# Scaled operands left in pieces between later products, with T2 and T4 kept negated, in a two-level Winograd graph layer

## The chip, the cores and the metric

The kernel runs on one core of a Trainium2 chip. The metric is the device time in microseconds (us) of one execution; lower is better. The profile is of a single execution, taken by the hardware profiler. Five engines work beside each other: TensorE (PE, with its weight loads as PEld), VectorE (DVE), ScalarE (ACT), GpSimd (POOL) and SyncE (SP). Each works through its own instructions in order, and semaphores hold an instruction until what it needs is there. In this kernel SP issues loads, and POOL issues stores and a few small loads besides its own sums.

## The reference

Two graph layers on x (4096 x 512) with one matrix adj (4096 x 4096), all in float32:

```
# layer 0
mask = (adj > 0); head = mask / max(sqrt(row sum of mask), 1e-12)
inc  = adj + head
x1   = layernorm(x + (inc @ x) / rowsum(inc))
# layer 1
A2   = adj + I;  d = diag(A2) ** -0.5
temp = A2 @ x1 @ W.T
out  = layernorm(x1 + relu(d * (A2 @ (d * temp))))
```

So there are three large products (inc @ x, A2 @ x1 and A2 @ (d * temp)) and one small one, the projection by W.T, which stands between the second and the third.

## The kernel before, in words

**Large products.** Layer 0 uses Winograd's form of Strassen's scheme on one level, and the two products with A2 use it on two levels. The code numbers them k = 2 (A2 @ x1) and k = 3 (A2 @ (d * temp)). On the outer level the left matrix is cut in quarters and the right matrix, 4096 x 512, in quarters B11, B12, B21, B22 of 2048 x 256. Seven outer products p = 1 to 7 are made, for each of two column stretches s of the result (s = 0, 1), in the order of `ORDER` (L179): 4, 5, 1, 6, 7, 2, 3 for k = 2 and 2, 3, 5, 1, 6, 7, 4 for k = 3. Each outer product takes one right operand out of seven (`OPERAND`, L181): B11, B21, B22 or one of the sums

```
T1 = B11 - B12      T2 = -T1 - B22      T3 = B22 - B12      T4 = B21 + T2
```

The right operands lie in HBM, in the tiles `outer_b[k]`, until `load_b` (L247) fetches them in groups for two steps; `sum_b` (L253) makes the inner sums of a group.

**Steps.** An outer product is eight steps, kk = 0 to 7. A step is seven inner products (`multiply2`, L273), each of four matmuls of 128 x 512 and each into its own PSUM bank (0 to 6); the eighth bank is the spare. The main loop (L993 to L1061) emits, for each step: the left sums for the step two later (`prepare`, on DVE), every second step the right sums (`sum_b`, DVE), pieces of the projection, the seven products, loads, and what follows the products. After kk = 7, `outer` (L701) evicts the seven banks by way of `inner` (L680): ACT copies bank q1 to p1 (L684) and q5 to p5 (L687), DVE does the rest (L685 to L692) and adds into the outer results c11, c12, c21, c22. The next outer product writes the same banks again from its first step on, so its first inner product needs the copy L684 and its second one needs L685.

**Projection.** When half of the rows of A2 @ x1 (h = 1 or h = 0) is complete for a stretch s, four calls of `project` (L750) are put in the list `pairs`, and they are worked off two in each of the next two outer products. A call handles two row blocks of 128 rows (r = 0 and 1). The first call of an outer product starts at kk = 2 (here "the early block"), the second at kk = 4 ("the late block"). Each makes seven small products with W in the spare bank (L766), put between the inner products of a step; ACT copies each out (L768) before the next can start, since there is only one spare bank. POOL makes the sums of the left side (L773 to L776). The early block has its small products in the steps kk = 2, 3 and 4, the late block in 4, 5 and 6. Then DVE adds them up (L795 to L801) into two tiles `z` (a ring of two, one for each row block, holding `first` and `second`, the left and right half of the 512 columns) and into one tile `t` (a single buffer) with t = first - second of both row blocks (L804). The late block of an outer product writes the same two `z` and the same `t` that the early block had.

**Leaving.** `leave_operands` (L809) scales `first`, `second` and `t` by d on ACT (L816) and stores them from POOL (L819, L826) as right operands of k = 3. The rows of h = 1 come first: they write B21 and B22, and T2, T3, T4 with what of them comes from these rows. The rows of h = 0 come later: they write B11 and T1, and accumulate their part into T2, T3 and T4 in HBM. Both row blocks leave at once, right after the DVE sums: after kk = 4 for the early block and after kk = 6 for the late block. A block of h = 1 takes six scalings and eight transfers, a block of h = 0 eight scalings and ten transfers. A second `t` place, `m`, holds the negated copy that T2 and T4 want.

**Order.** The schedule is written by hand: the engines run in the order in which the loop emits their instructions. Pools give a tile's buffer again only when all its readers are done, transfers that read it among them.

There are eight outer products with a pair of projection blocks in them. In this document they are E, F (h = 1, s = 0), A, B (h = 0, s = 0), G, H (h = 1, s = 1) and C, D (h = 0, s = 1), in the order of time E, F, A, B, G, H, C, D.

Of the kernel before, what the change touches and what calls it, by code (L numbers as in the profile page):

```python
# [10 lines left out]
AF = mybir.ActivationFunctionType  # L11
ALU = mybir.AluOpType

P = 128
# [6 lines left out]
B11, B21, B22, T1, T2, T3, T4 = range(7)  # L21
# [5 lines left out]
def tile_adj_resnorm_d2(  # L27
# [37 lines left out]
    nc = tc.nc  # L65
    N, D = x.shape
    H = D // 2
# [9 lines left out]
    NQ = NB // 4  # L77
    SW = 512
    NS = NQ * P // SW
    SB = SW // P  # L80
# [14 lines left out]
    def spare():  # L95
        return bank(7)
# [15 lines left out]
    dscale = const.tile([P, NB], F32, name="dscale")  # L112
    nscale = const.tile([P, NB], F32, name="nscale")
# [22 lines left out]
    def in_outer(k, j, ops):  # L136

        kk, half = j % NQ, j // NQ
        ap = outer_b[k][kk // 2][ops, kk % 2, :, 2 * half:2 * half + 2, :]
        return ap.rearrange("o p q d -> p o (q d)")  # L140

    def split(y):
        return y.rearrange("p (o d) -> p o d", o=2)
# [48 lines left out]
    completed = set()  # L192
    resident, loaded, ready, raw_b, sums_b = {}, {}, {}, {}, {}
    made = {"a": 0, "s": 0, "load": 0, "load_b": 0}
    going = []
    queue, pairs, later, deferred, raises = [], [], [], [], []

    def fresh():
# [102 lines left out]
    chunks, sums, slots, counts, scale, natural = {}, {}, {}, {}, {}, {}  # L301
# [328 lines left out]
    for n in range(NC, NP * NC):  # L630
        j, c = divmod(n, NC)
# [62 lines left out]
    def add(o, y):  # L694
        nc.vector.tensor_add(o, o, y)

    def less(o, y, z):

        nc.vector.scalar_tensor_tensor(o, y, -1.0, z, op0=ALU.mult, op1=ALU.subtract)

    def outer(k, p, acc):  # L701

        (c11, c12), (c21, c22) = C_of[k]

        def into(dst):
            inner(acc, lambda i, op: op(dst[:, i, :]))

        def by_way(then):
            def put(i, op):
                y = row_tile("y", 2)  # L710
                op(y)
                then(i, y)
            inner(acc, put)

        if k == 2:
            if p in (4, 5, 1):
                into({4: c21, 5: c22, 1: c11}[p])
            elif p == 6:
                into(c12)
                deferred.extend((lambda: add(c12, c11), lambda: nc.vector.tensor_sub(c21, c21, c12),  # L720
                                 lambda: add(c12, c22)))
            elif p == 7:
                into(c22)
                deferred.extend((lambda: nc.vector.tensor_sub(c21, c21, c22), lambda: less(c22, c22, c12)))
            else:
                dst = {2: c11, 3: c12}[p]
                by_way(lambda i, y: add(dst[:, i, :], y))
        else:
            if p in (2, 3):
                into({2: c11, 3: c12}[p])  # L730
            elif p == 5:
                into(c22)
                deferred.append(lambda: add(c12, c22))
            elif p == 1:
                into(c21)
                deferred.append(lambda: add(c11, c21))
            elif p == 6:
                by_way(lambda i, y: add(c21[:, i, :], y))
                deferred.append(lambda: add(c12, c21))
            elif p == 7:  # L740
                by_way(lambda i, y: add(c21[:, i, :], y))
                deferred.append(lambda: less(c22, c22, c21))
            else:
                by_way(lambda i, y: nc.vector.tensor_sub(c21[:, i, :], y, c21[:, i, :]))

    def blocks(h, s):

# [2 lines left out]
    def project(h, s, n, first):  # L750

        cols = slice(n * P, (n + 1) * P)
        a11, a12, a21, a22 = (C_of[2][h][f][:, 2 * r:2 * r + 2, cols] for r in range(2) for f in range(2))
        if first:
            pools["places"] = [t[:, i * H:(i + 1) * H] for t in (row_tile(t, 1) for t in ("p1", "p5", "u2", "u3")) for i in range(2)]

        places = [pools["places"][i] for i in (range(7) if first else (7, 1, 0, 6, 3, 2, 4))]
        q = []  # L760

        def product(left, right):
            def now():
                ps = spare()[:, 0:H]
                for e in range(2):
                    nc.tensor.matmul(ps, left[:, e, :], wt[:, right, e, :], start=(e == 0), stop=(e == 1))  # L766
                q.append(places[len(q)])
                nc.scalar.copy(q[-1], ps)  # L768
            return now

        def sums():
            s1, s2, s3, s4 = (y[:, 2 * i:2 * i + 2, :] for y in (row_tile("y", 2, (P, 4, P)) for _ in range(2)) for i in range(2))
            nc.gpsimd.tensor_add(s1, a21, a22)  # L773
            nc.gpsimd.tensor_add(s2, a11, s1)
            nc.gpsimd.tensor_add(s3, a11, a21)
            nc.gpsimd.tensor_add(s4, a12, s2)  # L776
            return s1, s2, s3, s4

        if first:
            yield {1: product(a11, B11), 3: product(a12, B21), 5: product(a22, T4)}  # L780
            s1, s2, s3, s4 = sums()
            yield
            yield {1: product(s2, T2), 3: product(s3, T3), 5: product(s1, T1)}
            yield
            yield {1: product(s4, B22)}
        else:
            yield {4: product(a11, B11)}
            s1, s2, s3, s4 = sums()
            yield
            yield {1: product(a12, B21), 3: product(a22, T4), 5: product(s2, T2)}  # L790
            yield
            yield {1: product(s3, T3), 3: product(s1, T1), 5: product(s4, B22)}
        q1, q2, q4, q6, q7, q5, q3 = q
        z = [row_tile("z", 2) for _ in range(2)]
        nc.vector.tensor_add(z[0][:, 0:H], q2, q1)  # L795
        nc.vector.tensor_add(q6, q6, q1)
        nc.vector.tensor_add(q7, q7, q6)
        nc.vector.tensor_add(q6, q6, q5)
        nc.vector.tensor_add(z[0][:, H:D], q3, q6)
        nc.vector.tensor_sub(z[1][:, 0:H], q4, q7)  # L800
        nc.vector.scalar_tensor_tensor(z[1][:, H:D], q7, -1.0, q5, op0=ALU.mult, op1=ALU.subtract)  # L801
        t = row_tile("t", 1, (P, 4, H))
        for r in range(2):
            nc.vector.tensor_sub(t[:, 2 * r, :], z[r][:, 0:H], z[r][:, H:D])  # L804
        for r in range(2):
            leave_operands(h, r * NQ + s * SB + n, z[r], t[:, 2 * r, :], t[:, 2 * r + 1, :])
        yield

    def leave_operands(h, j, z, t, m):  # L809

        b = j + h * NP

        def scaled(o, y, by=dscale):
            nc.scalar.activation(o, y, AF.Copy, scale=by[:, b:b + 1])  # L816

        def put(op, y, **how):
            nc.gpsimd.dma_start(out=in_outer(3, j, slice(op, op + 1)), in_=y.unsqueeze(1), **how)  # L819

        first, second = z[:, 0:H], z[:, H:D]
        if h:
            scaled(m, second, nscale)
            scaled(z, z)
            scaled(t, t)
            nc.gpsimd.dma_start(out=in_outer(3, j, slice(B21, B22 + 1)), in_=split(z))  # L826
            put(T2, m)
            put(T3, second)
            put(T4, t)
        else:  # L830
            scaled(m, t, nscale)
            scaled(t, t)
            scaled(first, first)
            scaled(second, second, nscale)
            put(B11, first)
            put(T1, t)
            put(T2, m, accum_op=ALU.add)
            put(T3, second, accum_op=ALU.add)
            put(T4, m, accum_op=ALU.add)

    def turn_back(ps, at, h, r, cols, fs):

# [52 lines left out]
    def finish(h, items, acc):  # L895


        c21 = C_of[3][h][0]
# [11 lines left out]
        def put(i, op):  # L910
            y = row_tile("y", 2)
            op(y)
            nc.vector.tensor_sub(c21[:, i, :], y, c21[:, i, :])

        def turn(t):
            j, r, cols = items[t]
# [76 lines left out]
    for n, (k, s, p, kk) in enumerate(steps):  # L993
# [15 lines left out]
        between = {3: lambda: take_up(items.pop(0))} if len(items) > 1 else {}  # L1009
        if kk in (2, 4) and pairs:  # L1010
            going.append(project(*pairs.pop(0), kk == 2))
        for pair in going:
            between.update(next(pair))
        if n < len(steps) - TAIL:
            multiply2(n, acc, between)
        if n == 0:
# [15 lines left out]
            next(pair)  # L1032
        if kk in (4, 6):
            del going[:1]
        if 1 <= kk <= (6 if end else 5):
            for kind, args in queue[:2]:
                fetch(kind, *args)
        if kk == NQ - 1 and n + 1 < len(steps):
            outer(k, p, acc)
            if (k, p) in DONE:  # L1040
                h = DONE[k, p]
# [8 lines left out]
                fetch(kind, *args)  # L1050
        while raises:
            raises.pop(0)()
        if n + 1 == len(steps) // 2:

            scope.close()
            ring3 = ctx.enter_context(tc.tile_pool(name="ring3", bufs=2))
            late["pool"] = ctx.enter_context(tc.tile_pool(name="late", bufs=1))
            i = made["a"] % 4
            pools["turn"] = [ring3] * 2 + pools["turn"][i:] + pools["turn"][:i]
            made["a"] = 0  # L1060
            PF = 3  # L1061
# [36 lines left out]
```

## Time and profile before

| What | Value |
|---|---|
| median of three executions | 2285.16 us (2283.39 to 2285.18) |
| the profiled execution, its own time | 2284.03 us |
| its span, first to last instruction | 2282.1 us |
| granted TensorE clock, mean | 0.998 |
| PE busy | 2255.1 us, 99% |
| DVE busy | 1854.4 us, 81% |
| ACT busy | 417.3 us, 18% |
| POOL busy | 383.3 us, 17% |
| moved by DMA | 555.80 MB, mean 244 GB/s |
| outer products with a projection | from 1058 to 1682 us |

The profile counts an engine as busy while it executes, and "idle before" is the time for which it stood still before an instruction, with the one that released it behind the arrow. PE is busy nearly throughout, so a time is changed only by what makes PE stand still, or by what takes matmuls away. A time on another engine counts only where PE, in the end, waits for it.

### The profile page before, as it was taken

Reading aid. Unit: us, or ns where it says so; the run is one execution under the profiler, and the core shown is the slowest. Engines: PE = TensorE matmul, PEld = TensorE weight load, DVE = VectorE, ACT = ScalarE, POOL = GpSimd, SP = SyncE. Lnnn points to the kernel's source line nnn. Section 1 sums busy time; section 2 is a strip of 40 time slices with the busy share of each in tenths; the row PEclk is TensorE's granted clock in tenths of the full one; section 3 lists DMA queues with packets and bytes.
Section 4 is the critical chain, followed back from the end, with each engine's and each line's share of the span. In section 5 each row is a group of like instructions: output and inputs, shape, how many; then the busy total and the mean of one; then the engine's idle time right before and its main releaser. Section 6 shows DMA issues by size and latency. Waiting matters only on the chain.

```text
span 2282.1 us, 22004 instructions
## 1 busy us (share of the span) xinstructions
PE 2255.1 (99%) x7359; PEld 1380.3 (60%) x7359; DVE 1854.4 (81%) x2619; ACT 417.3 (18%) x991; POOL 383.3 (17%) x548
## 2 busy tenths in 40 slices
PE   8999999999999999999999999999999999999997
PEld 6888888888888844444555444555544444444443
DVE  6988988988988777788876778887666788776788
ACT  4333223332232000000222100122110011100013
POOL 0111112211111110001333300232320000100013
PEclk9999999999999999999999999999999999999999
DMA  9788777878777576575767857576785676766573
GB/s 330 274 287 262 260 233 270 272 262 270 238 240 239 187 266 259 198 283 184 270 240 227 262 209 271 191 283 261 209 256 218 220 258 241 253 238 227 209 269 117
DMA packets 155936, 555.80 MB, mean 244 GB/s; under 512 B 17920, under 2 KB 32272, under 8 KB 117424
## 3 DMA queue, kind: packets, MB, share of 16 engines
q1 hardware_dynamic: 114624, 417.38, 51.6%
q0 software_dynamic: 41200, 137.03, 18.2%
q8 instruction: 58, 0.95, 0.2%
q14 instruction: 54, 0.44, 0.1%
HBM read 434.78 MB, written 119.55 MB: 243 GB/s over the span
## 4 chain that ended last, share of the span: by engine, by line
PE 89%; DVE 5%; DMA 3%; ACT 2%; issue 1%; POOL 0%; SPq 0%; DVEq 0%; ACTq 0%
PE q L278 55%; PE q L472 27%; PE q L766 3%; PE q L485 2%; DMA nat<-adj 2%; DVE s L167 1%; PE q L908 1%; PE q L844 1%; DVE s L169 0%; ACT z L816 0%; ACT nat L332 0%; DVE a L442 0%; DVE mask L435 0%; ACT t L816 0%; DVE ts L257 0%
## 5 line engine op out<-in xcount | busy, mean ns | idle before, releaser
L278 PE MATMUL q<-s,ts 128*128 128x512 f32 x1326 | 612.2, 592 | 0.1
L472 PE MATMUL q<-b,s 128*128 128x256 f32 (+1 forms) x1920 | 454.4, 379 | 0.0
L278 PEld LDWEIGHTS q<-s,ts 128*128 128x128 f32 x1326 | 251.6, 190 | 299.1 <-issue 268.3
L167 DVE TENSOR_TENSOR s<-a 128x1024 f32<-128x1024 f32 x236 | 290.2, 1230 | 161.4 <-PE q L278 131.3
L472 PEld LDWEIGHTS q<-b,s 128*128 128x128 f32 x1920 | 363.1, 189 | 53.1 <-DVE z L510 0.5
L472 PE MATMUL q<-b,a 128*128 128x258 f32 (+1 forms) x1440 | 352.5, 380 | 0.7 <-ACT p L503 0.6
L278 PE MATMUL q<-a,tr 128*128 128x512 f32 x692 | 329.4, 592 | 1.8 <-DMA a<-adj_r 1.8
L472 PEld LDWEIGHTS q<-b,a 128*128 128x128 f32 x1440 | 272.5, 189 | 40.9 <-ACT p L503 1.5
L278 PE MATMUL q<-s,tr 128*128 128x512 f32 x442 | 225.7, 592 | 0.0
L278 PEld LDWEIGHTS q<-a,tr 128*128 128x128 f32 x692 | 129.5, 190 | 145.1 <-issue 138.9
L332 ACT ACTIVATE nat<-nat,tiny 128x512 f32<-128x512 f32 x240 | 170.9, 714 | 235.9 <-DMA nat<-adj 235.7
L278 PE MATMUL q<-a,ts 128*128 128x512 f32 x346 | 176.8, 592 | 0.0
L169 DVE TENSOR_TENSOR s<-a,s 128x512 f32<-128x512 f32 x236 | 167.7, 711 | 8.1
L170 DVE TENSOR_TENSOR s<-a,s 128x512 f32<-128x512 f32 x236 | 167.3, 709 | 8.0
L442 DVE TENSOR_TENSOR a<-a,mask 128x1024 f32<-128x1024 f32 x123 | 150.7, 1225 | 6.6 <-DVE mask L435 0.5
L435 DVE SCALAR_TENSOR_TENSOR mask<-a,sc 128x1024 f32<-128x1024 f32 (+2 forms) x129 | 154.1, 1196 | 2.1
L278 PEld LDWEIGHTS q<-s,tr 128*128 128x128 f32 x442 | 84.0, 190 | 92.1 <-issue 84.6
L684 ACT COPY p<-q 128x512 f32<-128x512 f32 x27 | 15.6, 577 | 631.5 <-PE q L278 631.5
L278 PEld LDWEIGHTS q<-a,ts 128*128 128x128 f32 x346 | 65.7, 190 | 83.0 <-issue 76.1
L425 POOL DMA_DIRECT2D oa<-sr x64 | 57.7, 902 | 283.8 <-DVE sr L416 181.6
L873 POOL DMA_DIRECT2D out<-o x24 | 13.1, 547 | 507.8 <-ACT o L162 507.8
L278 PE MATMUL q<-r,tr 128*128 128x512 f32 x192 | 92.7, 593 | 0.0
(193 smaller groups left out, 2129.4 us busy)
## 6 DMA issues: line engine op xcount, KB each, us to landing
a<-adj_r SPq DMA_DIRECT2D x112, 1024.0 KB, 6.6
a<-oa SPq DMA_DIRECT2D x80, 1024.0 KB, 5.3
nat<-adj SPq DMA_DIRECT2D x240, 256.0 KB, 7.4
a<-adj_q SPq DMA_DIRECT2D x60, 1024.0 KB, 6.2
tr<-ob SPq DMA_DIRECT2D x112, 512.0 KB, 4.0
oa<-sr POOLq DMA_DIRECT2D x64, 512.0 KB, 7.2
oa<-r POOLq DMA_DIRECT2D x32, 1024.0 KB, 9.2
y<-x POOLq DMA_DIRECT2D x64, 256.0 KB, 7.2
```

Source lines behind the costliest of these rows:

```text
L167: nc.vector.tensor_add(s[:, S3:S1 + 1, :], a[:, A11:A22 + 1, :], a[:, A21, :].unsqueeze(1).to_broadcast([P, 2, w]))
L169: nc.vector.tensor_add(s[:, S2, :], a[:, A11, :], s[:, S1, :])
L170: nc.vector.tensor_add(s[:, S4, :], a[:, A12, :], s[:, S2, :])
L278: nc.tensor.matmul(acc[m], left, right, start=(kk == 0), stop=(kk == NQ - 1))
L332: nc.scalar.activation(y, a, AF.Sign, bias=tiny, scale=2.0 ** 64, accum_out=accum)
L425: nc.gpsimd.dma_start(out=dst, in_=sr.rearrange("p m (k i) -> p (m k) i", i=P))
L435: nc.vector.scalar_tensor_tensor(m, v, 0.0, s.unsqueeze(1).to_broadcast(list(v.shape)), op0=ALU.is_gt, op1=ALU.mult)
L442: nc.vector.tensor_add(z, z, y)
L472: nc.tensor.matmul(acc[m][:, 0:w], left, b[:, right, 0:w], start=(kk == 0), stop=(kk == NP - 1))
L485: nc.tensor.matmul(y[:, 0:w], left, slots[kk][:, op, 0:w], start=(kk == 0 and left is k1), stop=(kk == NP - 1 and left is k2))
L766: nc.tensor.matmul(ps, left[:, e, :], wt[:, right, e, :], start=(e == 0), stop=(e == 1))
L844: nc.tensor.transpose(ps[:, at + i * P:at + (i + 1) * P], C_of[3][h][d // 2][:, 2 * r + d % 2, cols], ident)
```

## The change

The scaling and the transfers are taken out of the projection's last piece and put in a list, `leaving`, with one entry for each row block. An entry is taken off at four places of the loop: during kk = 5 and during kk = 7 ahead of the seventh inner product, after kk = 5, and at the end of kk = 7 behind `outer`. So the early block leaves in and after kk = 5 instead of after kk = 4, and the late block in kk = 7, with its second row block behind the eviction of the banks, instead of after kk = 6.

T2 and T4 are stored with the opposite sign. Then `second` serves T2 and T3 of h = 1 as it is, and `t` serves T1, T2 and T4 of h = 0 as it is: the negated copy `m` and its scaling go, and one transfer with a repeated source writes two operands. A block of h = 1 has four scalings and six transfers, a block of h = 0 six scalings and eight transfers (seven for two row blocks, one of each half). The bytes of the operands stay the same. Where the outer products p = 6 and p = 4 of k = 3 are added up, the sign is taken back: an addition becomes a subtraction, and y - c becomes -y - c.

```diff
-    going = []
+    going, leaving = [], []
 ...
             elif p == 6:
-                by_way(lambda i, y: add(c21[:, i, :], y))
+                by_way(lambda i, y: nc.vector.tensor_sub(c21[:, i, :], c21[:, i, :], y))
 ...
             else:
-                by_way(lambda i, y: nc.vector.tensor_sub(c21[:, i, :], y, c21[:, i, :]))
+                by_way(lambda i, y: less(c21[:, i, :], y, c21[:, i, :]))
 ...
-        for r in range(2):
-            leave_operands(h, r * NQ + s * SB + n, z[r], t[:, 2 * r, :], t[:, 2 * r + 1, :])
+        leaving.extend(lambda r=r: leave_operands(h, r * NQ + s * SB + n, z[r], t[:, 2 * r, :]) for r in range(2))
         yield
 
-    def leave_operands(h, j, z, t, m):
+    def leave_operands(h, j, z, t):
 ...
-        def scaled(o, y, by=dscale):
-            nc.scalar.activation(o, y, AF.Copy, scale=by[:, b:b + 1])
+        def scaled(y, by):
+            nc.scalar.activation(y, y, AF.Copy, scale=by[:, b:b + 1])
 
-        def put(op, y, **how):
-            nc.gpsimd.dma_start(out=in_outer(3, j, slice(op, op + 1)), in_=y.unsqueeze(1), **how)
+        def put(ops, y, **how):
+            o = in_outer(3, j, ops)
+            nc.gpsimd.dma_start(out=o, in_=y.unsqueeze(1).to_broadcast([P, o.shape[1], H]), **how)
 
         first, second = z[:, 0:H], z[:, H:D]
         if h:
-            scaled(m, second, nscale)
-            scaled(z, z)
-            scaled(t, t)
+            scaled(z, dscale)
+            scaled(t, nscale)
             nc.gpsimd.dma_start(out=in_outer(3, j, slice(B21, B22 + 1)), in_=split(z))
-            put(T2, m)
-            put(T3, second)
-            put(T4, t)
+            put(slice(T2, T3 + 1), second)
+            put(slice(T4, T4 + 1), t)
         else:
-            scaled(m, t, nscale)
-            scaled(t, t)
-            scaled(first, first)
-            scaled(second, second, nscale)
-            put(B11, first)
-            put(T1, t)
-            put(T2, m, accum_op=ALU.add)
-            put(T3, second, accum_op=ALU.add)
-            put(T4, m, accum_op=ALU.add)
+            scaled(t, dscale)
+            scaled(first, dscale)
+            scaled(second, nscale)
+            put(slice(T1, T1 + 1), t)
+            put(slice(B11, B11 + 1), first)
+            put(slice(T2, T4 + 1, 2), t, accum_op=ALU.add)
+            put(slice(T3, T3 + 1), second, accum_op=ALU.add)
 ...
@@ finish, put @@
-            nc.vector.tensor_sub(c21[:, i, :], y, c21[:, i, :])
+            less(c21[:, i, :], y, c21[:, i, :])
 ...
@@ main loop @@
         for pair in going:
             between.update(next(pair))
+        if kk in (5, 7) and leaving:
+            between[6] = leaving.pop(0)
         if n < len(steps) - TAIL:
             multiply2(n, acc, between)
 ...
         if kk in (4, 6):
             del going[:1]
+        if kk == 5 and leaving:
+            leaving.pop(0)()
 ...
         while raises:
             raises.pop(0)()
+        if kk == NQ - 1 and leaving:
+            leaving.pop(0)()
```

## The prediction

> **What bounds the kernel now.** I read the page first, then the waits of TensorE, then the timelines of single stretches.
>
> ```profile
> PE 2255.1 (99%) x7359; PEld 1380.3 (60%) x7359; DVE 1854.4 (81%) x2619; ACT 417.3 (18%) x991; POOL 383.3 (17%) x548
> PE 89%; DVE 5%; DMA 3%; ACT 2%; issue 1%; POOL 0%; SPq 0%; DVEq 0%; ACTq 0%
> PE q L278 <- DMA a<-adj_r: 1.8, 1, 1.8
> PE q L766 <- ACT p L768: 4.3, 8, 0.9
> ```
>
> PE is the bound, and the change takes no matmul away. The last line is what it can win: eight times, once in each outer product with a projection, a small product waits for ACT's copy out of the spare bank. The timelines of PE and ACT in kk = 5 of product A:
>
> ```profile
> 1207.19 1.02 PE L278 MATMUL q<-s,ts 128*128 128x512 f32 x2
> 1208.96 1.13 PE L766 MATMUL q<-wt,c 128*128 128x256 f32 x4 [0.74 <-ACT p L768]
> 1208.15 0.49 ACT L816 ACTIVATE z<-z,nscale 128x256 f32<-128x256 f32 x1
> 1208.55 0.35 ACT L768 COPY p<-q 128x256 f32<-128x256 f32 x1
> 1212.70 0.37 ACT L768 COPY u<-q 128x256 f32<-128x256 f32 x1 [2.21 <-PE q L766]
> ```
>
> The copy at 1208.55 stood behind eight scalings. PE's products otherwise start 0.86 us apart; here it took 1.77, and the next start came 0.10 late: 1.01 us lost where the column says 0.74. The eight waits sum to 4.3; with 0.27 more for each, 6.5 us are lost. 1212.70 is the last copy of kk = 5.
>
> What the change could cost is on DVE, later in A, and in the transfers:
>
> ```profile
> 1217.68 0.42 DVE L795 TENSOR_TENSOR z<-p,u 128x256 f32<-128x256 f32 x1
> 1221.71 0.42 DVE L799 TENSOR_TENSOR z<-u,u 128x256 f32<-128x256 f32 x1 [2.15 <-ACT u L768]
> 1222.05 0.42 DVE L800 TENSOR_TENSOR z<-p,p 128x256 f32<-128x256 f32 x1
> 1222.72 0.75 DVE L804 TENSOR_TENSOR t<-z 128x256 f32<-128x256 f32 x2
> 1225.37 0.69 DVE L170 TENSOR_TENSOR s<-r,s 128x512 f32<-128x512 f32 x1
> 1227.31 0.69 DVE L685 TENSOR_TENSOR c<-q,p 128x512 f32<-128x512 f32 x1 [1.25 <-ACT p L684]
> ```
>
> L795, L800 and L804 are where the late block writes the first `z`, the second `z` and `t`, whose buffers the early block's transfers must have left. For the ten transfers of A's early block (issued 1206.81 to 1211.88) and of its late block (1225.84 to 1230.84), issue to landing, and the queues from 1206 to 1222:
>
> ```profile
> DMA to landing us min/median/max: 2.0/4.1/9.5
> DMA to landing us min/median/max: 2.1/10.6/12.0
> q0 software_dynamic: 1056, 1.31, 51.9%
> q1 hardware_dynamic: 492, 2.18, 36.2%
> ```
>
> The slowest is the last: all ten have landed at 1221.4, 14.6 us after the first issue, and 1.3 us before L804. The late block's need 16.8.
>
> **The rule.** [...] from 1214 to 1222 the DMA engines' busy share reads 1.05, and transfers of 128 KB that took about 2 us alone took up to 9.5 there and 12.0 in the late set. [...]
>
> **The change part by part.**
>
> *Scalings behind the copies.* In kk = 5 the early block's scalings come behind the third copy. The eight waits go: -6.5 us. Nothing takes their place there: from the third copy to kk = 6's first (1212.70 to 1216.14) there are 3.4 us, and six scalings at 0.42 us apart take 2.5.
>
> *Fewer scalings and transfers.* 32 of each go (16 blocks, two each). Beyond the waits they are worth nothing: ACT is busy 18%, POOL 17%. A transfer with two operands in it issues in 0.72 us (L826) against 0.54 for one. The bytes stay, so the DMA work stays: 1056 packets, 8.3 us of all 16 engines in the early set (51.9% of 16 us), 6.8 us by the same view of the late set; I take 7.5.
>
> *The sign.* L743 exchanges one tensor operation for another; L744 and L913 become scalar-tensor-tensor ones, which take 0.69 to 0.71 us in that size (L692) against 0.69 (L695) and 0.79 (L913). Nothing, at most 0.4 us either way at the end.
>
> *The early block leaves later.* In A the wait's end moves PE 1.01 us earlier, so the third copy is at 1211.7; the first scaling ends at 1212.55 and the first issue follows 0.3 us later as before: 1212.85, against 1206.81. All of the slack is gone and more: L804 wants `t` at 1221.7, 8.9 us after that issue, and all eight sets of ten before took 13.4 to 17.9 us (13.4, 13.9, 14.6, 15.6, 15.8, 15.8, 16.8, 17.9). Worse, the loads of kk = 6 (a right group and two left tiles; one left tile in C and D, with another at kk = 7) now start with these transfers instead of 7 us behind them. By work: 7.5 us for the transfers, 6.8 for these loads (their share of each microsecond from 1214 to 1224, added up), 1.1 from issue to first packet: 15.4. In C and D it is 7.5 + 4.2 + 1.1, then up to 3 of the next load. I take 15.2 for all four.
>
> *What that stops.* DVE waits at L795 for the first `z`, then at L800 and L804 for the last transfers. Behind them stand the left sums of the next-but-one step and then L685, which empties the bank of the next outer product's second inner product. ACT's scalings for the late block stand ahead of L684, which empties the first bank. From L800 to the end of L685 it is 1226.0 + 0.69 - 1222.05 = 4.65 us without the wait for ACT. With L the landing and N the start of the next outer product's first inner product, its second can start at L + 4.70 instead of N + 0.86, so PE loses L - N + 3.85 (the first bank's copy ends at about L + 3.1 and is never the later bound):
>
> - A: L = 1212.85 + 15.2 = 1228.05, N = 1228.83 - 1.01 = 1227.8: 4.1 us.
> - B: issue 1274.0, L = 1289.2, N = 1289.0; here L244 (2.29 us) also stands between, so +6.03: 6.25 us.
> - C: issue 1600.8, L = 1616.0, N = 1615.8: 4.05 us.
> - D: issue 1662.1, L = 1677.3, N = 1677.1: 4.1 us.
>
> Together 18.5 us. With 13.4 for the landing it is 11.3, with 17.9 it is 29.3.
>
> *E to H.* Rows of h = 1 are stored plainly, six transfers of 1.28 MB instead of eight. Before, sets that met loads were down 9.3 to 10.4 us after their first issue. In F the first issue comes at 1152.3; PE waits only if the last lands after 1163.9, that is 11.6 us later. So nothing there, with little to spare.
>
> *The late block.* Its first row block's scalings are two or three ahead of L684 instead of all six or eight: L684 came 1.25 us late for L685 in A, C and D. That gain lies under the stop above. Its transfers have over 25 us until the next early block.
>
> *POOL's order.* The stores L237 pass ahead of the late block's transfers of h = 1. Their `r` is ready, and nobody waits for these transfers soon: nothing.
>
> Sum: -6.5 + 18.5 = +12.0 us on the profiled execution, 2284.03 to 2296.0. The median of the runs shown stands 1.1 above that execution, so the forecast is 2297.2.
>
> **Rivals.**
>
> *Faster.* The transfers land in time, since two issues are less and each double one is generated at once, and only the eight waits show: 2278.7. For it, POOL needs 1 to 2 us less for the set. Against it, the bytes are the same and the loads start at the same moment. It decides at the landing: with 12.2 us or less after the first issue the balance is negative, and no PE wait at all needs 11.1 (8.9 in B). No set of ten did that. Chance 0.13.
>
> *A draw.* Landings stay near 13.4 or below, or DVE's stop is partly covered by PE's own delay: stops of 4 to 11 us against 6.5: about 2285 to 2290, say 2287. Chance 0.12.
>
> *Heavier.* Landings of 17 us and more, and E to H stop as well (1 to 2 us each, being so near): 2308 and above, say 2312. Chance 0.09.
>
> That an edit does nothing at all is excluded for the waits: the order on ACT is what changes.
>
> **How the numbers follow.** The forecast's own chance is 0.66, with a range of its own from 2290 (13.4) to 2308 (17.9). The range of all goes from 2286, in the draw, to 2308: it leaves out the faster rival and most of the heavy one. Within 0.2% (4.6 us, about what a measurement of this kernel tells from no change) lies much of the draw: faster 0.13, same 0.09, slower 0.78.
>
> **What would show it.** Right: no wait of L766 for L768; new waits of DVE at L795, L800 or L804 for transfers `ob<-z` and `ob<-t`, only in A to D; PE waits of 4 to 6 us at L278 for ACT L684 and DVE L685 at the starts of four outer products, each following A to D; landings of L819 about 15 us after the first issue. Wrong: landings within 11 us; PE waits in E to H; or the eight waits still there.

## The result

The changed kernel takes 2300.74 us, the median of four runs (2298.02 to 2301.45), against 2284.95 us (2283.39 to 2285.18) for the kernel before on the same chip: a ratio of 1.0068, 95% interval 1.0054 to 1.0082. It is slower by 15.8 us; 12.0 were forecast, and the range was 2286 to 2308. The profiled execution took 2300.64 us, with a span of 2298.9.

One correction to the description of the kernel before: an inner product is one matmul of 128x128 by 128x512, not four; the profile records it as two, 0.86 us together.

Busy times and the chain that ended last, from the page of the changed kernel, and from its waits those of TensorE, with the time in total, the number and the longest:

```profile
PE 2262.1 (98%) x7358; PEld 1381.9 (60%) x7359; DVE 1854.1 (81%) x2619; ACT 400.6 (17%) x959; POOL 369.9 (16%) x516
PE 88%; DMA 5%; issue 3%; DVE 2%; POOL 1%; ACT 1%; SPq 0%; DVEq 0%; ACTq 0%; POOLq 0%
PE q L278 <- ACT p L684: 8.2, 4, 3.9
PE q L278 <- DVE c L685: 3.6, 4, 2.0
PE q L278 <- DVE y L685: 1.5, 2, 0.7
PE q L278 <- DVE u L686: 0.4, 2, 0.2
```

The eight waits of L766 are gone. In their place the inner products wait for the evictions of the outer product before, L684 on ACT and L685 and L686 on DVE, and the chain that ended last now has the transfers of the operands in it: `DMA ob<-z` holds 2% of it. What stops DVE is in its own waits, and the timeline behind A shows how it reaches PE (DVE, then ACT, then PE):

```profile
DVE z L795 <- DMA ob<-z: 43.5, 8, 9.7
DVE z L800 <- DMA ob<-z: 2.5, 4, 1.1
1228.06 0.42 DVE L795 TENSOR_TENSOR z<-p,u 128x256 f32<-128x256 f32 x1 [8.28 <-DMA ob<-z]
1230.68 0.43 DVE L800 TENSOR_TENSOR z<-p,p 128x256 f32<-128x256 f32 x1 [0.27 <-DMA ob<-z]
1231.36 0.75 DVE L804 TENSOR_TENSOR t<-z 128x256 f32<-128x256 f32 x2
1234.62 0.68 DVE L685 TENSOR_TENSOR c<-q,p 128x512 f32<-128x512 f32 x1
1231.86 0.51 ACT L815 ACTIVATE t<-t,dscale 128x256 f32<-128x256 f32 x1 [8.17 <-DVE t L804]
1233.07 0.56 ACT L684 COPY p<-q 128x512 f32<-128x512 f32 x1
1229.99 1.02 PE L278 MATMUL q<-a,ts 128*128 128x512 f32 x2
1233.69 1.12 PE L278 MATMUL q<-r,tr 128*128 128x512 f32 x2 [2.68 <-ACT p L684]
1235.35 1.59 PE L278 MATMUL q<-r,tr 128*128 128x512 f32 x2 [0.54 <-DVE c L685]
```

DVE wanted the first `z` at 1219.8, had it at 1228.06 and the second at 1230.68. The last transfer of A's early block landed at 1230.6, 14.8 us after the first issue (1215.80). PE's next two products would have started at 1230.85 and 1231.71; they started at 1233.69 and 1235.35, so the second is 3.64 us late.

The same execution shows something that the kernel before has only at its very end: a granted TensorE clock of one half, the state in which a product takes twice as long (its records start 0.85 us apart there and 0.43 otherwise). The stretches' columns are PE, PEld, DVE, ACT and POOL busy, then the clock, the DMA share and GB/s:

```profile
1225.00:1235.80 10.80, 7.58 (x17) 2.90 (x17) 7.08 (x14) 3.47 (x8) 2.44 (x5) 1.00 0.96 263
1235.90:1239.30 3.40, 3.40 (x5) 1.30 (x4) 3.09 (x5) 0.00 (x0) 3.40 (x6) 0.50 0.97 330
1300.70:1307.50 6.80, 4.80 (x6) 1.59 (x6) 6.42 (x10) 1.42 (x4) 5.98 (x7) 0.50 1.00 190
```

Behind A the half clock begins 2.2 us after PE has started again and lasts 3.4 us; behind B it lasts 6.8 us. (A third stretch of 3.4 us, from 61.69 us on, lies in the first layer, behind a wait of 2.0 us there.)

Where the time went, in all profiles: the small products (L766) mark each outer product with a projection, so the start of its first and of its last small product, each against the kernel before, tells what was won within it and what was lost between it and the next. Gains and losses in us:

| Profile | before E | in E to D, together | F to A | A to B | B to G | H to C | C to D | after D | span |
|---|---|---|---|---|---|---|---|---|---|
| changed kernel | +1.36 | -6.45 | +2.82 | +5.45 | +8.72 | +1.81 | +1.21 | +1.89 | +16.8 |
| again (r1) | -1.64 | -6.45 | +2.77 | +5.49 | +10.20 | +1.85 | +1.14 | +2.13 | +15.5 |
| again (r2) | -1.39 | -6.45 | +2.84 | +5.47 | +8.74 | +1.80 | +1.26 | +4.25 | +16.5 |
| e6, PE kept busy | +1.56 | -6.45 | +2.90 | +3.66 | +6.86 | +2.00 | +1.26 | +2.17 | +14.0 |
| e5, no accumulation | +1.00 | -6.45 | +3.90 | 0.00 | +0.41 | +2.18 | 0.00 | -0.02 | +1.0 |
| e2, only later | -1.48 | -6.45 | +3.55 | +4.95 | +8.22 | +2.34 | +8.03 | +8.75 | +27.9 |
| e9, split, old transfers | +1.59 | -6.45 | 0.00 | +0.76 | +4.98 | 0.00 | 0.00 | +0.38 | +1.3 |
| e1, at once | +1.48 | -1.95 | 0.00 | 0.00 | 0.00 | 0.00 | 0.00 | -0.01 | -0.5 |
| e7, split | +0.15 | -6.45 | 0.00 | 0.00 | 0.00 | 0.00 | 0.00 | -0.02 | -6.3 |

Between E and F and between G and H nothing is lost in any of them. The column "before E" is layer 0 and the first products of k = 2, which the change does not touch; it swings by 3 us between profiles of one and the same kernel. In the first profile the half clock at 61.69 us falls into it.

### The profile page after: what moved, and what is told of

Its sections match the earlier page's. It is cut to its first block, busy times and chain, and to the rows that moved or that the text cites. A ratio compares the mean times of both kernels' runs of the same rounds, so it can differ in the third digit from the quotient of the medians.

```text
span 2298.9 us, 21953 instructions
## 1 busy us (share of the span) xinstructions
PE 2262.1 (98%) x7358; PEld 1381.9 (60%) x7359; DVE 1854.1 (81%) x2619; ACT 400.6 (17%) x959; POOL 369.9 (16%) x516
## 4 chain that ended last, share of the span: by engine, by line
PE 88%; DMA 5%; issue 3%; DVE 2%; POOL 1%; ACT 1%; SPq 0%; DVEq 0%; ACTq 0%; POOLq 0%
PE q L278 52%; PE q L472 31%; PE q L766 3%; DMA ob<-z 2%; DMA nat<-adj 1%; DMA b<-x 1%; PE q L485 1%; PE q L904 1%; PE q L840 1%; POOL ob L819 0%; DMA a<-adj_r 0%; POOL y L774 0%; DMA a<-adj_q 0%; ACT nat L332 0%; DVE s L167 0%
## 5 line engine op out<-in xcount | busy, mean ns | idle before, releaser
L278 PE MATMUL q<-s,ts 128*128 128x512 f32 x1326 | 614.3, 594 | 0.5 <-DVE u L686 0.4
L278 PEld LDWEIGHTS q<-s,ts 128*128 128x128 f32 x1326 | 252.4, 191 | 302.3 <-issue 269.2
L167 DVE TENSOR_TENSOR s<-a 128x1024 f32<-128x1024 f32 x236 | 290.3, 1230 | 151.1 <-PE q L278 118.5
L278 PE MATMUL q<-a,tr 128*128 128x512 f32 x692 | 332.9, 596 | 10.4 <-ACT p L684 5.5
L278 PE MATMUL q<-s,tr 128*128 128x512 f32 x442 | 225.7, 592 | 0.0
L278 PEld LDWEIGHTS q<-a,tr 128*128 128x128 f32 x692 | 128.9, 190 | 157.7 <-issue 133.7
L278 PE MATMUL q<-a,ts 128*128 128x512 f32 x346 | 177.0, 593 | 0.0
L278 PEld LDWEIGHTS q<-s,tr 128*128 128x128 f32 x442 | 84.0, 190 | 92.1 <-issue 83.7
L684 ACT COPY p<-q 128x512 f32<-128x512 f32 x27 | 15.6, 577 | 631.5 <-PE q L278 631.5
L278 PEld LDWEIGHTS q<-a,ts 128*128 128x128 f32 x346 | 65.5, 190 | 83.7 <-issue 75.6
L278 PE MATMUL q<-r,tr 128*128 128x512 f32 x192 | 93.6, 596 | 3.2 <-ACT p L684 2.7
```

Source lines behind the costliest of these rows:

```text
L167: nc.vector.tensor_add(s[:, S3:S1 + 1, :], a[:, A11:A22 + 1, :], a[:, A21, :].unsqueeze(1).to_broadcast([P, 2, w]))
L278: nc.tensor.matmul(acc[m], left, right, start=(kk == 0), stop=(kk == NQ - 1))
```

## The experiments

The theory: the early block's transfers start so late that DVE must wait for `z` and `t`, and with DVE stand the evictions, so that PE stops at the start of the next outer product. Three rivals: the combined transfers themselves are slow; the scalings of the late block, which now stand ahead of L684, stop PE whatever the transfers do; a good part of the loss is the half clock.

**r1 and r2: the changed kernel again.** No edit.

> The changed kernel once more, as a mark for the three beside it. 2300.7 us was measured; I expect 2298 to 2302. By the theory (the early block's transfers leave too late, so that DVE stops for `z` and `t` and PE for DVE and ACT) its profile shows PE waits at L278 for ACT L684 and DVE L685 of 10 to 15 us together, behind A, B, C, D, F and H. In the first layer, up to 1050 us, the first profile was 1.4 us later than that of before, from landings of `nat`; if that is chance it changes here.

> The changed kernel again, as a mark on the same chip for the one with extra products: 2298 to 2302 us, with the granted clock at one half for 3 us or more behind A and for 7 to 10 us behind B.

Measured: 2299.40 us (ratio 1.0065, 1.0050 to 1.0080) and 2302.29 us (1.0075, 1.0060 to 1.0090). The stops come back at the same six places and in nearly the same sizes; behind B r1 loses 10.20 us, with 10.2 us of half clock instead of 6.8. What was 1.36 us late before E in the first profile is 1.64 and 1.39 us early here, so that part is chance. In r2 the clock is halved behind D also, and there the loss is 4.25 instead of 1.89.

**e1: the change without its delay.**

```diff
-        leaving.extend(lambda r=r: leave_operands(...) for r in range(2))
+        for r in range(2):
+            leave_operands(h, r * NQ + s * SB + n, z[r], t[:, 2 * r, :])
```

> The change without its delay: T2 and T4 negated, fewer scalings and transfers, but both row blocks leave right behind the DVE sums as before. Theory of the late transfers: six scalings instead of eight (four instead of six for h = 1) let the copy L768 at the start of kk = 5 go about 0.8 to 1 us earlier, so the eight waits of 4.3 us (6.5 us of lost time) nearly vanish, the first issues come about when they came before (1206.8 in A), and no new wait shows: 2278 to 2280 us. Rival, that the transfers with a repeated source are what costs: the landings of the ten-now-eight stay at 15 us or more and it is slower than before, 2290 to 2300.

Measured: 2281.49 us, ratio 0.9988 (0.9979 to 0.9997). No stop behind any outer product, and the combined transfers are not slow: A's eight landed 12.2 us after the first issue, B's 11.7, against 14.8 and 16.0 in the changed kernel, where they start with the loads of kk = 6. That rival falls. The time is above the expected band, since a wait of the old kind is left in F and in H, longer than before (lines of PE's waits, then of DVE and ACT ahead of F):

```profile
PE q L766 <- ACT p L768: 3.8, 2, 1.9
1123.00 2.29 DVE L236 TENSOR_TENSOR r<-r,a 128x2048 f32<-128x2048 f32 x1 [3.53 <-DMA a<-adj_r]
1147.88 0.72 ACT L816 ACTIVATE z<-z,dscale 128x512 f32<-128x512 f32 x1 [5.09 <-DVE t L804]
1149.92 0.35 ACT L768 COPY p<-q 128x256 f32<-128x256 f32 x1
```

Ahead of F, and again ahead of H, DVE waited 3.5 us for a left tile, so its sums for the early block were later, and so were the scalings and the copy behind them. No run tells why that load was late. What it shows is that, with all scalings ahead of the copy, a delay of this size on DVE reaches PE.

**e2: the delay alone.** The kernel before, with its own `leave_operands` and its negated copy, called from the list at the four places of the change.

```diff
-            leave_operands(h, ..., z[r], t[:, 2 * r, :], t[:, 2 * r + 1, :])
+        leaving.extend(lambda r=r: leave_operands(h, ..., z[r], t[:, 2 * r, :], t[:, 2 * r + 1, :]) for r in range(2))
```

> The delay alone: the scalings and transfers of the kernel before (with the negated copy), taken from the list `leaving` at the places of the changed kernel. Theory: the stops are there, and larger, as each block of h = 0 has ten transfers again and the first of them waits for the third scaling (0.85 us later): 3 to 5 us over the changed kernel, 2302 to 2308. Rival (the combined transfers cost): near the kernel before or faster, 2279 to 2286, as the eight waits go.

Measured: 2311.30 us, ratio 1.0114 (1.0099 to 1.0129), above the expected band:

```profile
PE q L278 <- ACT p L684: 20.6, 6, 6.2
```

Behind C and D, 8.0 and 8.8 us are lost where the changed kernel loses 1.2 and 1.9; in each, 6.8 us of half clock have come in. So the delay is what costs, and the fewer scalings and transfers take some 12 us off its price (2299.40 in r1, on the same chip).

**e7: the same transfers, left in two parts.** The first row block leaves right behind the DVE sums; the second leaves one step on, behind ACT's first copy.

```diff
         if kk in (5, 7) and leaving:
-            between[6] = leaving.pop(0)
+            between[2] = leaving.pop(0)
 ...
-        if kk == 5 and leaving:
+        if kk in (4, 6) and leaving:
             leaving.pop(0)()
 ...
-        if kk == NQ - 1 and leaving:
-            leaving.pop(0)()
```

> The changed kernel with another place for the leaving: the first row block right behind the DVE sums (kk = 4 and 6), the second ahead of the third inner product of the next step (kk = 5 and 7), so that the copy of the first small product goes between them on ACT. Theory: first issues as before (about 1206.5 in A), the second row block's about 1.5 us later than before; the eight waits go (6.5 us), and the last landing, 1222 to 1223 in A, costs DVE about 1 us, which its slack of 1 to 2 us covers except in B: 2278 to 2281. Rival (any leaving in the step with later products stops DVE): 2285 or more.

Measured: 2277.91 us, ratio 0.9974 (0.9963 to 0.9986): faster than both kernels. On ACT, in kk = 5 of A, the copy has its place between the two row blocks:

```profile
1204.87 0.49 ACT L815 ACTIVATE z<-z,nscale 128x256 f32<-128x256 f32 x1
1205.59 0.37 ACT L768 COPY p<-q 128x256 f32<-128x256 f32 x1 [0.23 <-PE q L766]
1205.86 0.51 ACT L815 ACTIVATE t<-t,dscale 128x256 f32<-128x256 f32 x1
```

Three scalings fit in ahead of it, with 0.23 us to spare, and the other three before the next copy at 1208.12. All eight waits are won and nothing is lost behind; DVE does not wait for a transfer at L795, L800 or L804, where about 1 us was expected in A. The sets of A to D landed 12.0, 12.3, 13.4 and 14.8 us after a first issue that, relative to PE, is some seven us earlier than the changed kernel's (in A 1204.86 against 1215.80, of which about 4 are PE's own lead).

**e9: e7's places with the transfers of the kernel before.** The same three edits on e2.

> The kernel before with its own scalings and transfers (negated copy, ten and eight transfers), left in two parts as in the fastest kernel so far: the first row block right behind the DVE sums, the second ahead of the third inner product of the next step. If the gain there is only a matter of when ACT's copy gets its turn, this one gains as much: 2277 to 2279. If the fewer transfers and scalings are needed for it, it gains less: 2280 to 2285.

Measured: 2282.72 us, ratio 0.9991 (0.9982 to 1.0000). The waits go here too, but B's ten transfers landed 19.1 us after their first issue instead of e7's 12.3 with eight, and `t` came late there (DVE, then the waits of PE):

```profile
1283.48 0.42 DVE L801 SCALAR_TENSOR_TENSOR z<-p 128x256 f32<-128x256 f32 x1
1287.54 0.76 DVE L804 TENSOR_TENSOR t<-z 128x256 f32<-128x256 f32 x2 [3.64 <-DMA ob<-t]
PE q L278 <- ACT p L684: 3.3, 2, 2.8
```

Behind B the clock is halved for 3.4 us as well. So the negated T2 and T4 are of use, as what makes room for the later second part; this rests on one profile of e9, whose execution took 2285.29 us, above the median.

**e5: the changed kernel with less to transfer.** The two accumulating `put` of h = 0 are left out.

> The changed kernel without the accumulating transfers: the part of the h = 0 rows in T2, T3 and T4 is left out, so a block of h = 0 has four transfers instead of eight (the scalings stay). Places of leaving as in the changed kernel. Theory of the held buffers: the early sets of A to D have landed within 9 us of their first issue, DVE waits at L795 for less than 3 us and PE not at all behind A to D, the half clock goes too, and only F (2.8) and H (1.8) are left of the stops: 2284 - 6.5 + 4.6 = 2281 to 2283. Rival (the order on ACT, with scalings ahead of L684, stops PE whatever the transfers do): stops behind A to D of 3 us and more stay, 2290 or more.

Measured: 2284.93 us, ratio 1.0003 (0.9993 to 1.0012); the span is 1.0 us over that of the kernel before, of which 1.0 lies before E. The early sets of A to D landed within 7.9 to 9.2 us, and DVE waited there at L795 for 3.0 to 3.8 us, just over the expected 3. Of the stops behind A to D one of 0.41 us is left, behind B; those of F and H stay, and with them what is left of PE's waits:

```profile
PE q L278 <- DVE y L685: 1.5, 2, 0.7
PE q L278 <- ACT p L684: 1.1, 2, 0.9
```

The time is over the expected 2281 to 2283, as the clock was halved for 3.4 us behind F, which lost 3.90 us instead of 2.82. The scalings ahead of L684 were not touched, so the order on ACT alone does not stop PE: that rival falls.

**e6: PE kept busy while it stands still.**

```diff
+        idle = {(5, 0): 3, (1, 0): 4, (1, 1): 2}
         for m, (right, left) in enumerate(factors(n)):
+            for _ in range(idle.get((steps[n][2], m), 0) if steps[n][:2] == (2, 1) and kk == 0 else 0):
+                nc.tensor.matmul(spare(), ident, wt[:, B11].rearrange("p e d -> p (e d)"), start=True, stop=True)
```

> The changed kernel with nine extra products (128x128 by 128x512, constant operands, into the spare bank, never read; 0.86 us each) ahead of the first inner product behind A (three) and behind B (four, and two ahead of the second inner product), where PE stands still. If the half clock is due to PE standing still and costs half of its length, the clock stays at 1.0 there, the same starts are late by the stop alone (3.6 us behind A, 7.0 behind B) and the whole takes 3 to 5 us less than the changed kernel in spite of the extra work: 2295 to 2297. If the half clock is nothing or comes anyway, the time is as the changed kernel's or up to 1 us more.

Measured: 2296.64 us, ratio 1.0050 (1.0035 to 1.0065), against 2302.29 for the changed kernel beside it: 5.6 us less in spite of nine products more. The stretches in which r2 has the half clock, first of r2, then of e6:

```profile
1233.20:1236.60 3.40, 3.40 (x6) 1.36 (x5) 3.11 (x5) 0.00 (x0) 3.40 (x6) 0.50 0.96 339
1298.10:1304.90 6.80, 4.72 (x6) 1.51 (x5) 6.42 (x10) 1.27 (x4) 5.83 (x7) 0.50 1.02 185
```

```profile
1233.20:1236.60 3.40, 3.17 (x8) 1.25 (x8) 3.23 (x6) 2.32 (x6) 2.70 (x6) 1.00 0.99 381
1298.10:1304.90 6.80, 6.54 (x15) 2.49 (x15) 6.42 (x9) 2.23 (x6) 6.78 (x9) 1.00 1.07 253
```

In e6 the granted clock is never halved before the last 9 us, and what is lost behind A and B falls from 5.47 and 8.74 to 3.66 and 6.86. So of the changed kernel's 15.4 us between E and the end, about 3.6 are the half clock behind A and B: a part of the loss, not the whole. The gain of 5.6 us is more than the expected 3 to 5; the rest lies behind D, where r2's profile, unlike those of the first run and r1, has a half clock too and loses 4.25 us against 2.17 in e6.

## Why the prediction was right, and where it was off

**The mechanism held in A to D.** DVE stops at L795 and L800 for the early block's transfers, and PE at L278 for L684 and L685. The rule that PE loses L - N + 3.85, with L the last landing and N the next outer product's natural start, gives for A 1230.6 - 1230.85 + 3.85 = 3.6; 3.64 was measured. For B, with 6.03, it gives 1297.4 - 1296.45 + 6.03 = 7.0; there 1304.35 against 1297.31 is 7.04. In C and D the forecast of 4.05 and 4.1, less what their landings fell short of 15.2, comes to 1.1 and 1.8; 1.21 and 1.89 were measured. Two of its signs came out otherwise: it named PE waits in E to H as a sign of being wrong, and they came in F and H; and DVE waits at L795 in all eight products, not only in A to D (1.2 and 1.1 us in E and G, 5.6 to 9.7 in the others). In E and G no left tile was loaded beside the early set (0.52 MB of loads in 7 us), which landed in 6.8 and 6.9 us, and PE lost nothing.

**The scalings behind the copies:** -6.5 forecast, -6.45 measured, in each of the three profiles.

**The sum of the stops:** 18.5 forecast, 21.9 in the first profile.

| Behind | Forecast | Measured | Of it half clock | What was off |
|---|---|---|---|---|
| A | 4.1 | 5.45 | 1.8 | landing 14.8 us instead of 15.2; the clock was not thought of |
| B | 6.25 | 8.72 | 1.7 | landing 16.0 instead of 15.2; the clock |
| C | 4.05 | 1.21 | 0 | landing 12.2 instead of 15.2 |
| D | 4.1 | 1.89 | 0 | landing 12.9 instead of 15.2 |
| F | 0 | 2.82 | 0 | landing 13.1 where 11.6 was taken as the limit |
| H | 0 | 1.81 | 0 | landing 12.2, likewise |

The half clock's part is the measured loss less that of the second product's start (3.64 and 7.04); e6 gives 1.8 and 1.9.

Three terms were mis-sized. In C and D the working said 7.5 + 4.2 + 1.1 "then up to 3 of the next load", and took nearly all of the 3; the sets were down before that load counted, and 7.5 + 4.2 + 1.1 = 12.8 was the right figure. And the step "E to H: nothing there, with little to spare" failed: its 9.3 to 10.4 us came from sets that had met their loads some 4 us after their own start. Set off together with the loads, the six plain transfers of F and H took 13.1 and 12.2 us, and in e1, ahead of the loads, 7.1 and 7.7. The argument that was made for A to D, that all work queued at one moment counts, was left out there. The limit of 11.6 us was too wide as well: F's own gain of 0.59 us moves N, as A's 1.01 did, so it was 11.0. By that the second product of F should be late by 2.1 us (measured 1.96) and that of H by 1.2 (0.96). The rest of their losses comes with the third bank: here the evictions go by way of `y`, so L695 stands between L685 and L686, and PE waits three times behind F:

```profile
1168.85 1.12 PE L278 MATMUL q<-a,tr 128*128 128x512 f32 x2 [0.81 <-ACT p L684]
1170.70 1.13 PE L278 MATMUL q<-a,tr 128*128 128x512 f32 x2 [0.73 <-DVE y L685]
1172.03 2.84 PE L278 MATMUL q<-s,ts 128*128 128x512 f32 x6 [0.20 <-DVE u L686]
```

The third term is the half clock, 3.5 us, which the forecast had at nothing. Some 5 us too much for C and D stand against some 8 too little for F, H and the clock. That these cancelled in part, and the total came out within the range at 21.9 - 6.45 = 15.4, is luck; this profile adds 1.4 from before E.

**The wait at the first `z`.** I had the last landing decide. In the trace DVE's long wait is at L795, for the first `z`, and L800 adds only 0.3 to 1.1 us. It made little difference to the sum: the first `z` came free 2.3 to 3.5 us before the second, and L795 to L799 take 2.4.

**The loads in a landing.** The forecast counted the loads of SP in a landing of POOL's, and in five of the six products compared that held: the same six or eight transfers took 7.1 to 12.2 us ahead of the loads in A, B, C, F and H (e1) and 12.2 to 16.0 beside them. In D it was the other way, 14.6 in e1 and 12.9 here; no run tells why. The queues behind A show the sharing. From 1218 to 1226 us the loads (q1) and the transfers (q0) run together, from 1226 to 1230 the loads are done:

```profile
q1 hardware_dynamic: 425, 2.37, 79.8%
q0 software_dynamic: 249, 0.42, 23.4%
q0 software_dynamic: 764, 0.89, 116.0%
q1 hardware_dynamic: 10, 0.00, 0.4%
```

Beside the loads the transfers' queue moved 31 packets per us, alone 191.

## What to carry to other kernels

When work is put off to clear one engine's queue, look at what buffers it holds and who writes them next: here the list of deferred work was free on ACT and POOL, and was paid on DVE and PE, which waited for the one set of `z` and `t` that there is (no run gave them a second one). Put off only what stands in the way (e7: one of two row blocks, past one copy), and start transfers ahead of the loads that will share the DMA engines with them (1.2 to 6.0 us sooner down in five of the six products compared here, later in one). A stop of the matmul engine can cost more than its length, because the clock may follow: here 5.45 us behind A for a stop of 3.64, with 3.4 us at half clock.

## What was not expected of the hardware

In these runs the granted clock fell to one half after stops of PE that are short. In the changed kernel it fell behind a pair of waits of 2.68 and 0.54 us (3.4 us at half clock) and behind one of 3.87 us, with another of 2.00 us soon after (6.8 us, in r1 10.2), in e5 behind waits of 0.92 and 0.73 us (3.4 us), and in e9 behind a single one of 2.83 us (3.4 us); it did not fall behind 0.81, 0.73 and 0.20 us in the changed kernel's F, nor behind single waits of 1.83 us for a load in the kernel before and of 1.92 us in e1. So the length of a stop alone did not decide.

In the trace of the changed kernel the half clock begins at 61.69, 1235.88, 1300.73 and 2290.60 us. From one beginning to the next it is 344, 19 and 290 times 3.413 us, and the first three stretches last 3.413, 3.413 and 6.827 us. In the trace of the kernel before it begins once, at 2271.52 us. With these two traces cut into pieces of 3.413 us, placed so that the half clock begins with a piece, PE stood still for 1.98, 1.76, 3.16 and 2.49 us in the pieces ahead of the four beginnings, and for 2.07 us ahead of the one in the kernel before. In no other piece at full clock from 12 us on was it more than 1.85 us (PE's ends are modelled, so that these figures are rough). The piece with 1.85 us, from 2283.77 us on in the changed kernel, was not followed by half clock, the one with 1.76 was, so the two cases overlap. The wait of 1.83 us for a load lay in two pieces, with 0.96 and 0.94 us of standing still, and the clock stayed at 1.00. That a stop costs more when it falls into one piece than when it is shared by two is an estimate from these figures; no run tried it.
